# Turning the scan's normalised rows over DRAM and VectorE instead of TensorE and ScalarE, from batch 3 on

## The chip, the cores and the metric

The kernel runs on one core of one Trainium2 chip. A core has TensorE (PE in the profile, its weight loads PEld), VectorE (DVE), ScalarE (ACT), GpSimd (POOL) and SyncE (SP), which here only issues transfers. The metric is the device time of one execution in microseconds (us); less is better.

## The reference

All numbers are float32; x has 8 batches of 512 tokens of 256 features. Four blocks follow each other, each on a layer norm and added back to x. Cut to what matters:

```python
def _layernorm(x, axis=-1, eps=1e-05):
    m = jnp.mean(x, axis=axis, keepdims=True)
    v = jnp.var(x, axis=axis, keepdims=True)
    return (x - m) / jnp.sqrt(v + eps)
...
def _L0_attn_a_ref(x, Win, bin_, Bp, Cp, Dp, Wout, bout):   # the scan
    xi = jax.nn.silu(x @ Win + bin_)
    def step(h, xt):
        h = h * DECAY + xt[:, :, None] * Bp[None, :, :]
        y = jnp.einsum('bij,ji->bi', h, Cp) + Dp * xt
        return (h, y)
    ...
    return y @ Wout + bout
...
x = x + _L0_attn_a_ref(_layernorm(x), ...)   # scan
x = x + _L0_ffn_ref(_layernorm(x), ...)      # shared experts, and 4 of 16 experts for each token
x = x + _L0_attn_b_ref(_layernorm(x), ...)   # causal attention, 16 heads
x = x + _L0_ffn_ref(_layernorm(x), ...)
```

The scan's product x @ Win sums over the 256 features, so on TensorE the normalised rows must stand with features on the partitions. That turning of rows is what this case is about.

## The kernel before, in words

The program has four stages, one after the other: a stretch of the scan with the router and the shared experts of the first mixture (0 to about 337 us in the profile), the routed experts of that mixture (to about 730), a stretch of the attention with the second mixture's router and shared experts (to about 1223), and the routed experts again.

A stretch (function stretch) runs over batches. Work is written as pieces, generators that yield how many TensorE columns each step takes. beside() interleaves pieces by their progress; timed() places steps of a piece at given fractions of the batch. This sets the order in which instructions are recorded; the build then lays each engine's instructions into a queue, which the engine works through in order. SP's transfers wait at the head of SP's queue in the same way.

In iteration b of the scan stretch stand side by side:

- main(b) of the scan: four products of the turned rows with Win (pz_s, L563), each followed by Silu on ScalarE (L572), the scan on VectorE (L574), a scaling on ScalarE (L575) and a VectorE sum (L578), then the product with Wout (py_s, L510) and the addition to x on VectorE (L519);
- for batch b − 1: the norm of the mixture (L468, L469, L487, L493 on VectorE, a power on POOL, L488), its turning on TensorE (pt_m, L430), the router's product (pl_m, L669), the choice of experts on VectorE (L695 to L784, with a product pr_m at L747), and, one batch later still, 16 scatters on POOL (L798), each ahead of which ScalarE makes one column of row numbers (L795);
- the shared experts of earlier batches: pg_m (L1146), Silu (L1164), a VectorE product (act_m, L1165), pd_m (L1174), a ScalarE copy (L1182) and a store on SP (L1184);
- for batch b + 1: the norm (steps at 0.32 to 0.44 and 0.56 to 0.64 of the batch) into a tile xn, and turn(b + 1), two steps at the fractions layer.turns;
- on SP the load of x for batch b + 2 (L149), six loads of expert weights and a store of zeros (L235 to L237, L348, L351), the store of x of batch b − 1 (L1444) and the store of the shared experts.

The first use of the turned rows of batch b + 1 is L563, at the start of iteration b + 1.

There are two ways to turn rows. turned() (L418) transposes each 128 x 128 block on TensorE against the identity into PSUM (pt_l, L430) and copies it to SBUF (L432), for the scan on ScalarE, one half of the features per step. by_shares() (L435) stores the rows to DRAM (L440), loads them back in four shares so that each 32 x 32 block stands in the partitions where it belongs (L443), all in its first step; in its second step VectorE transposes the 32 x 32 blocks in two halves (L452). Before the change by_shares is used in the attention stretch, from batch 2 on.

Of the kernel before, what the change touches and what calls it, by code (L numbers as in the profile page):

```python
# [82 lines left out]
def tile_hybrid_block(  # L83
# [334 lines left out]
    def turned(src, tag: str, into, copies, home=None, past=None):  # L418

        rows = src()  # L420
        if home is None:
            dst = work.tile([P, KD, T], FP, tag="kb4", name=f"xT_{tag}", bufs=KB)
        else:
            dst = home(f"xT_{tag}")
        into(dst)
        for k in range(KD):
            pt = bank([P, NT, P], f"pt_{tag}_{k}")
            for t in range(NT):
                with tc.issue_after(past[-1].ins) if past else nullcontext():
                    nc.tensor.transpose(pt[:, t, :], rows[:, t, :].rearrange("p (q k) -> p k q", k=KD)[:, k], ident)  # L430
            flat = pt.rearrange("p t q -> p (t q)")
            copies[k](dst[:, k, :], flat)  # L432
            yield T // 2

    def by_shares(src, tag: str, into, into_rows: bool, home=None):  # L435


        rows = src()
        through = dram.tile([T, D], FP, name=f"through_{tag}")
        nc.sync.dma_start(out=through.rearrange("(t p) d -> p t d", p=P), in_=rows)  # L440
        share = rows.rearrange("p t d -> p (t d)") if into_rows else kb4(f"share_{tag}").rearrange("p t d -> p (t d)")
        for a in range(QUAD):
            nc.sync.dma_start(  # L443
                out=share[a * SQ : (a + 1) * SQ, :].rearrange("s (g c) -> s g c", g=T // SQ),
                in_=through[:, a * KD * SQ : (a + 1) * KD * SQ].rearrange("(g s) c -> s g c", s=SQ),
            )
        yield 0
        dst = home() if home else work.tile([P, KD, T], FP, tag="kb4", name=f"xT_{tag}", bufs=KB)
        into(dst)
        for half in range(2):  # L450
            g = slice(half * T // SQ // 2, (half + 1) * T // SQ // 2)
            nc.vector.transpose(  # L452
                dst.rearrange("p k (g s) -> p k g s", s=SQ)[:, :, g],
                share.rearrange("p (g i k) -> p k g i", i=SQ, k=KD)[:, :, g],
            )
        yield 0

    by_both = (nc.scalar.copy, nc.vector.tensor_copy)
    by_scalar = (nc.scalar.copy, nc.scalar.copy)
# [60 lines left out]


    class Scan:
        mixture, ahead, copies, turns = 0, 1, by_scalar, (0.75, 0.79)
        quota = (10, 10, 20)
        over, sent, begun_last = 4, 0, 4
        early = 0


# [671 lines left out]
    class Attention:  # L1200
        mixture, ahead, copies, turns = 1, 2, by_both, (0.65, 0.85)
        quota = (10, 8, 20)
        over, sent, begun_last = 0, 4, 8
        early = 2
        norms, scores, choose = (0.0, 0.12, 0.2, 0.28), (0.29, 0.45, 0.55, 0.6), (0.66, 0.95)
        last_rows, last_scores = (0.2, 0.28), (0.35, 0.38)
# [214 lines left out]
    def stretch(layer):  # L1421


        i = layer.mixture
# [7 lines left out]
            return normed(b, f"l{i}_{b}", place, False, first)  # L1432

        def turn(b: int, copies=layer.copies):
            if i == 1 and b >= layer.ahead:
                return by_shares(lambda: xn.pop(b), f"l{i}_{b}", lambda xnT: xT.update({b: xnT}), True)
            return turned(lambda: xn.pop(b), f"l{i}_{b}", lambda xnT: xT.update({b: xnT}), copies)

# [20 lines left out]
        for b in range(layer.ahead):  # L1459
            if b < layer.early:  # L1460
                xT[b] = ready.pop(b)
            else:
                layer.load(b)
                first = i == 0 and b == 0
                issue(Piece(0, norm(b, first)))
                issue(Piece(0, turn(b)))
            if b == 0 and i == 1:
                issue(project(b))

        def first_two():  # L1470

            second = norm(1, True)
            issue(Piece(0, some(second, NT)))
            for _ in range(2):
                pending.pop(0)()
            issue(Piece(0, second))
            load_shared()
            with tc.issue_after(powers["l0_1"].ins):
                for make in late:
                    make()  # L1480
            layer.load(1)
            with tc.issue_after(powers["l0_1"].ins):
                issue(project(0))
            main = layer.main(0, made.pop(0))
            issue(Piece(0, some(main.steps, FIRST)))
            issue(Piece(0, turn(1)))
            issue(Piece(0, some(main.steps, NI - FIRST)))
            issue(project(1))
            second = layer.main(1, made.pop(1))
            issue(Piece(0, some(second.steps, NI)))  # L1490
            issue(main)
            keep_busy(5, "between")
            return Piece(second.columns - NI * KD * T, second.steps)
# [9 lines left out]
        for b in range(1 if begun else 0, B):  # L1503
# [3 lines left out]
            scores, choose, turns = layer.scores, layer.choose, layer.turns  # L1507
            if i == 0 and b == 1:

                scores, choose, turns = (0.95, 0.955, 0.97, 0.975), (0.98, 0.99), (0.96, 0.965)  # L1510
# [35 lines left out]
            if nxt < B:  # L1546
                added = layer.load(nxt)
                if added is not None:
                    pieces.append(timed(added, 0.31, 0.34))
                stats = 0.36 if added is not None else 0.32  # L1550
                pieces += [
                    timed(norm(nxt), *spread(stats, 0.44, NT), *spread(0.56, 0.64, NT)),
                    timed(turn(nxt), *turns),
                ]
# [133 lines left out]
```

## Time and profile before

| | us |
|---|---|
| median of 10 runs | 1616.78 (1612.17 to 1618.53) |
| the profiled execution's own time | 1619.3 |
| its span in the trace | 1617.6 |
| scan stretch, 0 to 340: PE busy / mean granted clock | 324.10 / 0.98 |
| routed experts, 340 to 730: PE busy / clock | 389.77 / 1.00 |
| attention stretch, 730 to 1225: PE busy / clock | 479.11 / 0.99 |
| routed experts, 1225 to 1617: PE busy / clock | 376.30 / 0.99 |

All times inside the kernel are of the profiled execution, counted from the start of its span. The profile names a line of the program by L and its number, and an operation by out<-in. In a timeline row stand the start, the length, the engine, the line, the operation and its tiles, how many were merged (x8), and in brackets how long the engine had been idle and who ended that. A product of the program appears as two to four matmuls there. The granted clock is the share of TensorE's full speed that the chip granted.

### The profile page before, as it was taken

How to read it: one execution, taken by the hardware profiler on the slowest of the kernel's cores; microseconds unless marked ns; L12 is line 12 of the kernel's file. 1: busy time of each engine (PE TensorE's matmuls, PEld its weight loads, DVE VectorE, ACT ScalarE, POOL GpSimd, SP SyncE). 2: the span in 40 equal slices, each digit the busy share in tenths (PEclk: the TensorE clock that was granted, in tenths of full speed). 3: DMA queues.
4: the chain of work that ended last, by engine and by line, in shares of the span. 5: the costliest groups of instructions: out<-in, count | busy, mean ns of one | idle time of the engine just before them, and what ended most of it. 6: DMA issues, size and time to landing. Idle time of an engine off the chain costs nothing. (4 is left out here: it accounts for less than half of the span.)

```text
span 1617.6 us, 34092 instructions
## 1 busy us (share of the span) xinstructions
PE 1569.3 (97%) x10030; PEld 1158.6 (72%) x10030; DVE 1003.1 (62%) x3264; ACT 779.4 (48%) x1622; POOL 771.9 (48%) x639
## 2 busy tenths in 40 slices
PE   8899999999999999999899999999999999999996
PEld 5466665689999999983354454544558999999995
DVE  6877765444466444437888888878844444545453
ACT  3343443245555555546554554454224555555553
POOL 4376655635556555550014422433533555555554
PEclk9999999999999999999999999999999999999998
DMA  5354423557777766641233434342745767777776
GB/s 171 120 202 148 153 104 133 185 92 106 121 123 105 107 97 98 95 66 40 79 89 99 141 96 119 101 123 98 276 146 92 108 115 128 120 137 132 137 133 135
DMA packets 282766, 196.88 MB, mean 122 GB/s; under 512 B 168689, under 2 KB 262673, under 8 KB 282577
## 3 DMA queue, kind: packets, MB, share of 16 engines
q1 hardware_dynamic: 230016, 121.50, 29.0%
q0 software_dynamic: 51984, 72.09, 24.6%
q8 instruction: 85, 1.39, 0.4%
q10 hardware_dynamic: 576, 1.05, 0.2%
q14 instruction: 105, 0.85, 0.2%
HBM read 91.29 MB, written 103.23 MB: 120 GB/s over the span
## 5 line engine op out<-in xcount | busy, mean ns | idle before, releaser
L1073 POOL DMA_INDIRECT part<-rows x272 | 426.3, 1567 | 341.6 <-ACT rows L1072 260.1
L798 POOL DMA_INDIRECT xg<-sorted_m,slots_m x256 | 269.0, 1051 | 246.1 <-ACT slots_m L795 120.6
L1033 PEld LDWEIGHTS ph<-rows,gate 128*128 128x128 f32 x2160 | 277.6, 191 | 32.7 <-ACT rows L1016 22.6
L1033 PE MATMUL ph<-rows,gate 128*128 128x128 f32 x2160 | 291.7, 278 | 0.5 <-ACT rows L1016 0.5
L1033 PE MATMUL ph<-rows,up 128*128 128x128 f32 x2160 | 285.3, 275 | 0.0
L1063 PE MATMUL pyr<-w_all,rows 128*128 x1088 | 279.5, 380 | 1.4 <-DVE rows L1043 1.4
L1033 PEld LDWEIGHTS ph<-rows,up 128*128 128x128 f32 x2160 | 262.9, 192 | 0.0
L1006 DVE COPY up<-w_all 128x512 f32 x270 | 119.9, 445 | 226.3 <-PE ph L1033 210.9
L1006 ACT COPY gate<-w_all 128x512 f32 x270 | 166.4, 617 | 124.2 <-PE ph L1033 120.3
L1043 DVE TENSOR_TENSOR rows<-ph,rows 128x256 f32<-128x256 f32 x272 | 115.4, 424 | 155.2 <-PE ph L1033 142.1
L1295 ACT ACTIVATE w_all<-ps_a 128x1024 f32<-128x1024 f32 x160 | 155.2, 1021 | 105.4 <-PE ps_a L1285 101.3
L1063 PEld LDWEIGHTS pyr<-w_all,rows 128*128 128x128 f32 x1088 | 186.7, 192 | 15.8 <-DVE rows L1043 1.6
L1072 ACT ACTIVATE rows<-pyr,gain 128x256 f32<-128x256 f32 x272 | 128.6, 473 | 78.5 <-PE pyr L1063 61.9
L1041 ACT ACTIVATE rows<-ph 128x256 f32<-128x256 f32 x272 | 104.3, 383 | 117.2 <-PE ph L1033 106.2
L1174 PE MATMUL pd_m<-sd_sb,act_m 128*128 128x256 f32 x512 | 119.7, 383 | 2.2 <-DVE act_m L1165 1.3
L1174 PEld LDWEIGHTS pd_m<-sd_sb,act_m 128*128 128x128 f32 x512 | 96.1, 190 | 26.4 <-issue 8.8
L1285 PE MATMUL ps_a<-w_all 32*128 32x384 f32 (+3 forms) x1024 | 103.4, 467 | 11.5 <-ACT w_all L1295 11.4
L1305 DVE SCALAR_TENSOR_TENSOR w_all<-w_all,causal 128x512 f32<-128x512 f32 (+1 forms) x160 | 91.7, 573 | 26.4 <-ACT w_all L1295 25.5
L1146 PE MATMUL pg_m<-w_all,sg_sb 128*128 128x512 f32 x192 | 92.6, 604 | 0.0
L1146 PE MATMUL pg_m<-w_all,su_sb 128*128 128x512 f32 x192 | 92.6, 605 | 0.0
L1285 PEld LDWEIGHTS ps_a<-w_all 32*128 32x128 f32 x1024 | 45.1, 186 | 66.1 <-ACT w_all L1295 37.5
L1321 PE MATMUL po_a<-w_all,v_a 128*32 128x512 f32 (+3 forms) x1024 | 89.3, 449 | 0.0
(222 smaller groups left out, 1915.5 us busy)
## 6 DMA issues: line engine op xcount, KB each, us to landing
rows<-xg SPq DMA_DIRECT2D x720, 32.0 KB
rows<-xg SPq DMA_DIRECT2D x92, 134.0 KB
part<-x SPq DMA_DIRECT2D x16, 512.0 KB
w_all<-in_L_ffn_gate_w_dram SPq DMA_DIRECT2D x29, 256.0 KB
w_all<-in_L_ffn_up_w_dram SPq DMA_DIRECT2D x29, 256.0 KB
w_all<-in_L_ffn_down_w_dram SPq DMA_DIRECT2D x29, 256.0 KB
part<-ys_m SPq DMA_DIRECT2D x14, 512.0 KB
sum<-part SPq DMA_DIRECT2D x14, 512.0 KB
```

Source lines behind the costliest of these rows:

```text
L798: nc.gpsimd.indirect_dma_start(out=xg[i], out_offset=bass.IndirectOffsetOnAxis(ap=slots[:, at : at + 1], axis=0), in_=rows[:, t, :], in_of ...
L1006: copy(here, w_all[:, bass.ds(held[n][0] + half * KD * F, KD * F)])
L1033: nc.tensor.matmul(ph[s][:, f * P : (f + 1) * P], lhsT=both[s][:, k * F + f * P : k * F + (f + 1) * P], rhs=rows[:, ROW + k * P : ROW + (k ...
L1041: nc.scalar.activation(act, ph[0], AF.Silu)
L1043: made = nc.vector.tensor_mul(act, ph[1], act)
L1063: nc.tensor.matmul(py, lhsT=act[:, f * P : (f + 1) * P], rhs=w_all[:, bass.ds(w + 2 * KD * F + f * D, D)], start=(f == 0), stop=(f == KF - 1),
L1072: nc.scalar.mul(y, py, gain[:, TK : TK + 1])
L1073: acc = nc.gpsimd.indirect_dma_start(out=parts[i][n % 2], out_offset=bass.IndirectOffsetOnAxis(ap=rows[:, D + 2 * TK : D + 2 * TK + 1].bit ...
L1146: made = nc.tensor.matmul(dst, lhsT=w[:, k, f * P : (f + 1) * P], rhs=xnT[:, k, :], start=(k == 0), stop=(k == KD - 1),)
L1174: nc.tensor.matmul(py[:, j, :], lhsT=acts[n][:, f, t * P : (t + 1) * P], rhs=shared[n][3][:, f, :], start=(n == 0 and f == 0), stop=(n == ...
L1285: nc.tensor.matmul(ps[j // 2][:, j % 2, col : col + n], lhsT=k_sb[w][r, o, c * P : (c + 1) * P], rhs=q_sb[r, o, c * P : T], start=True, st ...
L1295: nc.scalar.activation(es[two], ps[two], AF.Exp, scale=ATT_SCALE)
```

## The change

Class Scan gets turns (0.66, 0.92) in place of (0.75, 0.79), and both classes an attribute through, the first batch that goes over DRAM: 3 for the scan, 2 for the attention, where it was layer.ahead = 2 before. So nothing changes in the attention. In the scan, batches 3 to 7 (turned in iterations 2 to 6) use by_shares: the store and the four loads at 0.66 of the iteration, the VectorE transposes at 0.92. The shares are loaded into the tile xn itself (into_rows is True). Batches 0 to 2 are turned as before; the turns of batch 2 have fractions of their own.

```diff
     class Scan:
-        mixture, ahead, copies, turns = 0, 1, by_scalar, (0.75, 0.79)
+        mixture, ahead, copies, turns = 0, 1, by_scalar, (0.66, 0.92)
         quota = (10, 10, 20)
         over, sent, begun_last = 4, 0, 4
+        through = 3
         early = 0
...
         over, sent, begun_last = 0, 4, 8
+        through = 2
         early = 2
...
         def turn(b: int, copies=layer.copies):
-            if i == 1 and b >= layer.ahead:
+            if b >= layer.through:
                 return by_shares(lambda: xn.pop(b), f"l{i}_{b}", lambda xnT: xT.update({b: xnT}), True)
             return turned(lambda: xn.pop(b), f"l{i}_{b}", lambda xnT: xT.update({b: xnT}), copies)
```

In the built program the queues of TensorE, ScalarE and SP differ only by the instructions that go or come, POOL's is the same. On VectorE some pairs of neighbours also change places (L519 and L739, L469 or L487 and L1165). The two VectorE transposes of batches 3 to 7 stand directly ahead of the first scan (L574) of their batch:

```
batch 4, VectorE's queue after the change
L731 pick_m_2<-sorted_m_2,numbers
L519 x<-py_s_1,x
L739 sel_m_2<-pick_m_2
L468 stats_m_3<-x (two)
L469 mv_m_3<-stats_m_3
L1165 act_m_1_1<-pg_m_1_1_1_1,sig_m_1_1_1
L469 mv_m_3<-stats_m_3
L487 rstd_m_3<-mv_m_3
L487 rstd_l_5<-mv_l_5
L452 xT_l_4<-xn_4 (two)
L574 state_s_0<-decay,xi_s_0
```

(Line numbers are those of the kernel before; the change adds a line each ahead of L526 and L1204.)

## The prediction, made before the result was known

> **What bounds the kernel now.** I read the page first: TensorE (PE) is busy through almost the whole span, no other engine is near it.
>
> ```profile
> PE 1569.3 (97%) x10030; PEld 1158.6 (72%) x10030; DVE 1003.1 (62%) x3264; ACT 779.4 (48%) x1622; POOL 771.9 (48%) x639
> ```
>
> An average over stages decides nothing about one of them, and the chain that ended last reaches back only to 1223 us, far behind the scan. So I took the windows of the scan, one for about each of the batches that change (us, then busy us of PE, PEld, DVE, ACT, POOL, granted clock, DMA share, GB/s):
>
> ```profile
> 100.00:125.00 25.00, 25.00 (x102) 15.10 (x101) 18.42 (x70) 12.04 (x30) 18.10 (x20) 1.00 0.56 187
> 125.00:150.00 25.00, 25.00 (x105) 15.98 (x104) 16.46 (x42) 10.69 (x27) 15.62 (x15) 1.00 0.47 160
> 150.00:175.00 25.00, 25.00 (x88) 15.41 (x87) 22.20 (x80) 9.78 (x24) 15.73 (x18) 1.00 0.31 109
> ```
>
> TensorE never stops here: from 77 to 210 us the list of waits has no PE wait. So TensorE time removed is time won, but every stop of TensorE that is added counts in full as well. Whether one is added is read where a batch ends. For batch 4 the timeline of PE gives (start, length, line):
>
> ```profile
> 118.34 1.11 PE L430 MATMUL pt_l<-ident,xn 128*128 128x128 f32 x8
> 119.29 1.89 PE L510 MATMUL py_s<-w_scan,y_s 128*128 128x256 f32 x8
> 121.02 1.88 PE L1146 MATMUL pg_m<-w_all,sg_sb 128*128 128x512 f32 x4
> 122.74 1.89 PE L510 MATMUL py_s<-w_scan,y_s 128*128 128x256 f32 x8
> 124.46 1.88 PE L1146 MATMUL pg_m<-w_all,su_sb 128*128 128x512 f32 x4
> 126.18 1.88 PE L563 MATMUL pz_s<-xT_l,w_scan 128*128 128x512 f32 x4
> ```
>
> The first row is what the change takes out; the last one, L563, is the first reader of the turned rows, 7.84 us later. At the same moment VectorE (DVE) does this:
>
> ```profile
> 124.43 0.58 DVE L739 TENSOR_REDUCE sel_m<-pick_m 128x64 f32<-128x256 f32 x1
> 124.93 0.68 DVE L519 TENSOR_TENSOR x<-py_s,x 128x512 f32<-128x512 f32 x1
> 125.64 0.75 DVE L468 BATCH_NORM_STATS2 stats_m<-x 128x6 f32<-128x256 f32 x2
> 126.31 0.30 DVE L469 BATCH_NORM_AGGREGATE mv_m<-stats_m 128x2 f32<-128x6 f32 x2
> 126.65 0.17 DVE L487 TENSOR_SCALAR rstd_m<-mv_m 128x4 f32<-128x4 f32 x1
> 126.73 0.69 DVE L1165 TENSOR_TENSOR act_m<-pg_m,sig_m 128x512 f32<-128x512 f32 x1
> 127.33 0.16 DVE L487 TENSOR_SCALAR rstd_l<-mv_l 128x4 f32<-128x4 f32 x1
> 128.82 1.23 DVE L574 TENSOR_TENSOR_SCAN state_s<-decay,xi_s 128x512 f32<-128x512 f32 x1 [1.32 <-ACT xi_s L572]
> ```
>
> It has no idle time from 116.83 to 127.49: the expert choice of the batch before, the sums and their statistics. TensorE is already in L563 by then. That is harmless now, and it is where I expect the change to hurt.
>
> **What goes.** Five batches (3 to 7) lose eight PE transposes and two ScalarE copies each. The transposes of batch 4 hold PE from 118.34 to 119.29, 0.95 us; the other batches' rows give the same. 5 x 0.95 = 4.75 us. The copies (group L432, 587 ns each, 5.9 us in all) are worth nothing: ScalarE is busy 10 to 12 us in 25, and no PE wait names it here.
>
> **What is added.** On VectorE two stream transposes per batch; the pair stands at 1.30 us in the attention stage (771.35), with the same tiles. On the SP queue a 512 KB store and four loads of 128 KB, each with its wait. Behind them on SP stand the store of x (L1444), in three batches the next stores and loads; L1444 waits for L519 (90.9 us in batch 3) anyway, so nothing there becomes late that TensorE reads.
>
> **Do the shares land in time?** The rows xn are complete at 110.76 in batch 4 (77.8, 146.1, 179.3, 213.1 in batches 3, 5, 6, 7). But SP has just issued eight transfers, some 2.2 MB (106.82 to 111.18), and the DMA share is 0.95 to 1.05 from 108 to 116, 0.35 after. I place the store behind that. From store to first load the attention stage needs 3.05 us on quiet queues (761.44 to 764.49) and 7.62 behind other loads (783.13 to 790.75); from first load to the end of the VectorE wait 4.9 (790.75 to 795.66). Batch 4: 116 + 3.05 + 4.9 = 124, or 111.2 + 7.62 + 4.9 = 123.7. VectorE comes to the transposes only at 127.5, so the transfer is hidden by 3.5 us. In batches 5 and 6 the share falls at 152 and 186, which gives 160 and 194, 2 to 3 us before VectorE. Batch 7 meets idle queues. Batch 3 is the tight one: the share stays high until 88, so 96 at the latest; 81.1 + 7.62 + 4.9 = 93.6 at the earliest. VectorE is free at 94.53 there, since the constants of L213 stand in front. I take 95.0.
>
> **Where VectorE's turn comes.** VectorE runs its queue in order, and the built program fixes it: in batches 4 to 6 the pair stands behind L519, L739, L468, L469, L1165 and both L487, directly ahead of the scan L574. L1165 itself needs the TensorE group directly ahead of L563 (batches 4 to 7). So TensorE finishes, waits for L1165, the small ones and the pair, and only then starts. Nothing stands between on TensorE's queue to fill it. With 1.30 us for the pair and 0.05 for the release, L563 starts:
>
> - batch 3: 95.0 + 1.35 = 96.35, was 92.11: +4.2
> - batch 4: 127.49 + 1.35 = 128.84, was 126.18: +2.7
> - batch 5: 162.88 + 1.35 = 164.2, was 160.28: +3.9 (here VectorE is slower by some 1.3 at 151.5 to 153.5, while POOL adds at L550; it may move)
> - batch 6: 195.76 + 1.35 = 197.1, was 194.37: +2.7
> - batch 7: 231.02 − 0.95, as L1165 waits for TensorE here, + 1.35 = 231.4, was 230.04: +1.4
>
> Sum +14.9, the 0.95 saved per batch already inside. VectorE's chain starts from TensorE's pl_m and py_s of the same batch, ahead of the removed row, so each batch pays anew and the shifts add.
>
> **The clock.** The idle time before L563 would be 5.2, 3.6, 4.9, 3.7 and 2.3 us. What follows an idle TensorE is in the trace (PE rows, then windows):
>
> ```profile
> 76.33 1.42 PE L430 MATMUL pt_m<-ident,sorted_m 128*128 128x128 f32 x6 [2.65 <-DVE sorted_m L493]
> 78.00:79.00 1.00, 1.00 (x2) 0.00 (x0) 0.00 (x0) 0.78 (x5) 0.69 (x2) 0.50 0.66 105
> 275.15 2.31 PE L430 MATMUL pt_m<-ident,sorted_m 128*128 128x128 f32 x8 [1.62 <-DVE sorted_m L493]
> 277.00:278.00 1.00, 1.00 (x4) 0.59 (x3) 0.00 (x0) 0.73 (x3) 0.00 (x0) 0.50 0.00 0
> ```
>
> After 2.65 us idle the clock is 0.50 from 77.8 to 81.2; after 1.62 us it is 0.50 from 275.8 to 279.2; after 1.31 us (210 to 211.3) it stays at 1.00; after 4.15 us (804.8 to 809.0) it is low from 808 to 815. Half speed for 3.4 us costs 1.7. Bounds: 0 per batch, and 3.4 (two such stretches). I take 1.5, nearest to the single stretch, part of which may fall into the idle time: 5 x 1.5 = 7.5.
>
> The Trainium skill, "TensorE: Matmul & The Clock Gate", section "HAM oscillation — how this bites in real kernels", tells to avoid PE idle gaps above about 3.4 us. By it only four of the five idle times would be punished and this term would be near 6.8; the 1.62 us row here shows a shorter one punished. The same page, "Part 4: PE-mode transpose", gives about 275 ns for a transpose in a kernel's context, by which an estimate of the saving would be 40 x 0.275 = 11 us; this trace has eight in 0.95 us, and that decides.
>
> **Sum.** +14.9 + 7.5 = 22.4. Back comes part of the 1.31 us at 210 (TensorE waits there for VectorE's L1165, which gains on a slowed TensorE), 0 to 1.3, taken as 0.7: +21.7. From 340 us on TensorE is full again (389.8 of 390 us) and nothing is changed, so the shift arrives at the end. The profiled execution took 1619.3 us (span 1617.6), giving 1641.0; it stands 2.5 above the median 1616.78, so the median becomes 1638.5.
>
> **Rivals.**
> - A, idle without a slow clock: the stops are as above, but TensorE keeps 1.00, as after the 1.31 us. 14.9 − 0.7: 1631. Against it: 1.62 and 2.65 us.
> - B, the shares land late: POOL's scatters use the DMA engines at the same time (POOL 15 to 18 us busy in 25), and if each round trip takes 7.62 + 4.9 after the burst instead of 3.05 + 4.9, the pair starts at 100.5 in batch 3 instead of 95.0, at 128.5, 164.5 and 198.5 in 4 to 6 instead of 127.5, 162.9 and 195.8: 5.5 + 1.0 + 1.6 + 2.7 = 10.8 more, 1649. For it: batch 3 has no margin at all.
> - C, faster: VectorE gets to the pair before TensorE gets to L563, then only the 4.75 us remain: 1612. It decides at 123.9 in batch 4 (125.23 − 1.35), 3.6 us before VectorE is free. The built queue speaks against it; only a VectorE much ahead of this trace would do it.
> - D, nothing measurable (within 0.2%, 3.2 us, about what this measurement can tell): stops of about 1 us each, which the 0.95 pays: 1617. It needs VectorE free 2.5 us earlier. That the change doesn't do what it says is excluded: the built program has 40 PE transposes and ten copies less, and ten VectorE transposes, five stores and twenty loads more.
>
> **Chances.** Forecast 0.64 (1632 to 1645), A 0.15 (1624 to 1632), B 0.12 (up to 1652), C 0.05, D 0.04. Range 1624 to 1650: it leaves out C, D and the end of B. Faster 0.05, same 0.04, slower 0.91.
>
> **What would show it.** Right: in the list of waits a new PE wait of L563 for DVE xT_l L452, five times, 2 to 5 us each, 17 to 20 in all; granted clock 0.50 for 3.4 us behind most of them; VectorE's L452 without a DMA wait in batches 4 to 7. Wrong: L452 waiting for DMA in all batches (B), L563 starting without idle time (C), or clock 1.00 throughout (A). The prediction falls if the batches' shifts don't add, that is if TensorE had slack behind L563 that the trace hides.

## The result, and the profile after

The changed kernel took **1641.56 us** (median of 8 runs, 1639.14 to 1643.71); the kernel before took 1616.71 beside it. The ratio is **1.0156, 95% interval 1.0147 to 1.0165**: slower by 24.9 us, where +21.7 was predicted. The profiled execution took 1638.05 us (span 1636.3). In the changed kernel L563 is L564, L574 is L575, L1165 is L1166.

The first line of the page shows that the intended removal happened (40 PE transposes less, ten ScalarE copies less, ten VectorE instructions more), and that PE was busy for longer all the same:

```profile
PE 1574.5 (96%) x9990; PEld 1156.1 (71%) x9990; DVE 1007.7 (62%) x3274; ACT 775.1 (47%) x1612; POOL 771.8 (47%) x639
```

Fewer instructions and more busy time mean slower instructions. Two of the three windows shown of before (PE, PEld, DVE, ACT, POOL, granted clock, DMA share, GB/s) show where:

```profile
125.00:150.00 25.00, 21.56 (x70) 13.15 (x69) 17.27 (x54) 6.99 (x18) 11.81 (x12) 0.93 0.24 78
150.00:175.00 25.00, 20.53 (x80) 12.30 (x80) 15.70 (x62) 7.01 (x20) 14.92 (x17) 0.89 0.70 233
```

PE stops for 3.4 and 4.5 us in windows where it never stopped, and the granted clock (third number from the end) falls below 1.00. The end of batch 4 in the timeline of PE:

```profile
126.36 1.88 PE L1147 MATMUL pg_m<-w_all,su_sb 128*128 128x512 f32 x4
131.68 2.82 PE L564 MATMUL pz_s<-xT_l,w_scan 128*128 128x512 f32 x3 [3.44 <-DVE xT_l L452]
```

L564 now waits 3.44 us for VectorE's transposes, and even then three of its matmuls take 2.82 us, where four took 1.88 before. VectorE in the same moments:

```profile
127.44 0.68 DVE L519 TENSOR_TENSOR x<-py_s,x 128x512 f32<-128x512 f32 x1
...
129.26 0.66 DVE L1166 TENSOR_TENSOR act_m<-pg_m,sig_m 128x512 f32<-128x512 f32 x1
...
130.22 1.30 DVE L452 STREAM_TRANSPOSE xT_l<-xn 128x512 f32<-128x512 f32 x2
```

No row carries an idle time in brackets: VectorE runs through, and the pair's turn comes last. The list of PE's waits from 60 to 300 us sums it up for the five batches (us, times, longest):

```profile
PE pz_s L564 <- DVE xT_l L452: 17.7, 5, 4.5
```

The single idle times are 4.46, 3.44, 4.47, 3.19 and 2.18 us (batches 3 to 7). Windows of 3.4 us from the start of each batch's first L564 show the clock, here batches 4 and 7:

```profile
131.70:135.10 3.40, 3.40 (x4) 1.38 (x5) 0.00 (x0) 0.00 (x0) 0.69 (x1) 0.51 0.00 0
...
249.10:252.50 3.40, 3.40 (x8) 1.54 (x9) 0.68 (x1) 0.69 (x1) 0.00 (x0) 1.00 0.02 5
```

Batches 3, 5 and 6 read 0.50 too. Four of the five stops are followed by half clock, four matmuls in the time of eight; behind the two longest it lasts on, to 97.6 and 176.1.

### The profile page after: what moved, and what is told of

It reads as the page before. It is cut to its first block, busy times and chain, and to the rows that moved or that the text cites. A ratio compares the mean times of both kernels' runs of the same rounds, so it can differ in the third digit from the quotient of the medians.

```text
span 1636.3 us, 34063 instructions
## 1 busy us (share of the span) xinstructions
PE 1574.5 (96%) x9990; PEld 1156.1 (71%) x9990; DVE 1007.7 (62%) x3274; ACT 775.1 (47%) x1612; POOL 771.8 (47%) x639
## 5 line engine op out<-in xcount | busy, mean ns | idle before, releaser
L1064 PEld LDWEIGHTS pyr<-w_all,rows 128*128 128x128 f32 x1088 | 186.8, 192 | 15.8 <-DVE rows L1044 1.6
```

The lines of the kernel that those rows point to most:

```text
L1064: nc.tensor.matmul(py, lhsT=act[:, f * P : (f + 1) * P], rhs=w_all[:, bass.ds(w + 2 * KD * F + f * D, D)], start=(f == 0), stop=(f == KF - 1),
```

## The experiments

Theories as in the prediction: **VectorE's queue** (the pair's turn comes late, TensorE stops, the clock falls), against **the transfer** (store and shares cost by landing late, B) and **no slow clock** (A). All variants differ from the changed kernel in the scan stretch only; added lines shift the numbers, so L564 appears as L568 to L579 and L452 as L455 to L463. The kernel before was timed beside each group, as chips differ: 1637.61 us for the first four runs, 1617.95 for the next four, 1616.77 for the last four. So ratios are compared, not times.

| run | median, us | ratio to before, 95% interval | as us |
|---|---|---|---|
| not turned at all | 1632.43 | 0.9967 (0.9954 to 0.9980) | −5.4 |
| transfer alone | 1645.20 | 1.0038 (1.0019 to 1.0056) | +6.2 |
| VectorE pair alone, late | 1655.90 | 1.0109 (1.0088 to 1.0131) | +17.9 |
| changed, idle time partly filled | 1656.41 | 1.0129 (1.0104 to 1.0154) | +21.1 |
| changed kernel again | 1642.24 | 1.0154 (1.0133 to 1.0175) | +24.9 |
| changed, idle time filled | 1632.10 | 1.0091 (1.0070 to 1.0112) | +14.7 |
| shares first and pair earlier | 1615.96 | 0.9989 (0.9976 to 1.0001) | −1.8 |
| rows early, pair in VectorE's gap | 1631.76 | 1.0086 (1.0065 to 1.0107) | +13.9 |
| shares first only | 1641.28 | 1.0146 (1.0125 to 1.0167) | +23.6 |
| pair earlier only | 1633.43 | 1.0098 (1.0078 to 1.0118) | +15.8 |
| from batch 6 on | 1624.59 | 1.0042 (1.0027 to 1.0058) | +6.8 |
| shares first, pair earlier, not batch 6 | 1613.16 | 0.9978 (0.9966 to 0.9990) | −3.6 |

The last column is (ratio − 1) times the group's kernel before.

### Not turned at all

```diff
+            if i == 0 and b >= layer.through:
+                return unturned(b)
```

(unturned gives L564 the tile xn as it lies)

> Batches 3 to 7 of the scan are not turned at all: TensorE's transposes, the copies, the store, the loads and VectorE's transposes are all left out, and L563 reads the normalised rows as they lie. It prices what the change removes. My theory (the wait for VectorE's queue costs everything, the removed transposes are worth 0.95 us a batch): 4.75 us under the kernel before, so about 1612 (1610.5 to 1613.5), no wait of L564 on TensorE's list and no half clock from 77 to 290 us. Rival (the gain is smaller since something else, such as VectorE's scores or act, ends the batch in any case): 1615 to 1617.

Measured −5.4 us (−7.5 to −3.3), and no wait of L564. The removed work is worth about what the prediction took, 4.75. Half clock was not gone altogether: 6.83 us of it stand from 254.17, behind a wait of 4.44 us of pr_m for sel_m that all four profiles of this group have (see the last section).

### The transfer alone

```diff
         yield 0
+        if tag[:3] == "l0_":
+            into(share.rearrange("p (k q) -> p k q", k=KD))
+            yield 0
+            return
```

> As the changed kernel, but VectorE's two transposes are left out in batches 3 to 7: the store and the four loads stay, and TensorE reads the loaded shares as they land. My theory (VectorE's queue position, not the transfer): TensorE waits only where the shares land behind it, in batch 3 (90.5 against 87.7 us, 2.8 idle and perhaps 1.7 of slow clock) and batch 5 (0.75): 1616.8 - 4.75 + 3.6 to 5.3 = 1615.6 to 1617.3. Rival, the transfer and what it crowds out on the DMA engines is the cost: about 1638 to 1642, as the changed kernel.

Measured +6.2 us (3.1 to 9.2): neither. The ten executions lie between 1638.2 and 1649.6 us, and the profiled one took 1648.9, so its waits may be above the typical ones. The waits of PE from 60 to 300 us:

```profile
PE pz_s L568 <- DMA xn<-through_l: 6.3, 2, 5.1
...
PE pd_m L1179 <- DVE act_m L1170: 3.7, 1, 3.7
```

In batch 3 TensorE waits 5.1 us for the shares, more than the 2.8 I had from the trace of after, and the wait for act_m (1.3 in the changed kernel) is 3.7: act_m stands in VectorE's queue behind a norm that waited 1.79 us for a scatter, until 215.91. That TensorE runs into this because nothing held it up earlier is argued, not tried. So the transfer alone is not the 25 us, but it is not free either.

### VectorE's pair alone, late

```diff
+        if tag[:3] != "l0_":
             nc.sync.dma_start(out=through.rearrange("(t p) d -> p t d", p=P), in_=rows)
...
+            if tag[:3] == "l0_":
+                behind_all(made)
```

(the four loads likewise; behind_all queues the pair behind the last 60 recorded instructions of VectorE)

> The other half alone: no store and no loads in batches 3 to 7, VectorE's two transposes read the normalised rows directly (so the rows between the quarters of partitions are not exchanged: that part of the turning is left out), and they are tied to the end of VectorE's queue, three small instructions (0.38 us) earlier than in the changed kernel in batches 4 to 7 and 2.7 us earlier in batch 3 (ahead of the constants of L213). My theory: idle before L564 is 4.46 - 2.7, 3.44 - 0.38, 4.47 - 0.38, 3.19 - 0.38, 2.18 - 0.38 = 13.5 us, slow clock 5 to 8 us, so 1633.5 to 1637. Rival, the transfer is the cost: 1612 to 1617, since no transfer is left.

Measured +17.9 us (14.4 to 21.5), with no store and no loads of the rows at all. The waits of PE:

```profile
PE pz_s L577 <- DVE mv_m L482: 11.6, 3, 4.6
...
PE pz_s L577 <- DVE xT_l L463: 2.7, 1, 2.7
...
PE pz_s L577 <- issue: 2.3, 1, 2.3
```

The same stop of the same line, 16.6 us in five waits (13.5 expected), named by other neighbours in VectorE's queue: in batch 4 the pair ends at 127.93 and L577 starts at 128.07. Most of the loss is there without a byte of the rows moved; the transfer theory falls as the main cause.

### TensorE's idle time filled, in part and wholly

```diff
+    FILL = {3: 15, 4: 11, 5: 15, 6: 10, 7: 6}     # second run: 17, 13, 17, 12, 8
...
+                if b in FILL:
+                    keep_busy(FILL[b], tag)
                 for c in range(NI):
```

> The changed kernel with 15, 11, 15, 10 and 6 fp32 matmuls of ones by ones (0.256 us each by the rows ahead of the second batch) put on TensorE directly ahead of the first L564 of batches 3 to 7, where it sits idle for 4.46, 3.44, 4.47, 3.19 and 2.18 us: 3.8, 2.8, 3.8, 2.6 and 1.5 us of work of no use, inside the idle time. Nothing else differs. My theory (the idle time is followed by half clock, 8.6 us in all): the waits stay, the half-clock stretches behind them go: 1641.6 - 8.6 = 1633 (1631.5 to 1635). Rival, the slow clock costs nothing or comes from something else than TensorE's idle time: 1641 or more.

> As the first run with matmuls of ones in TensorE's idle time, with more of them: 17, 13, 17, 12 and 8 ahead of the first L564 of batches 3 to 7 (4.4, 3.3, 4.4, 3.1 and 2.0 us), which leaves idle pieces under 1.5 us. In the first such run pieces of 2.05, 2.90 and 3.14 us were left, and two of the four half-clock stretches with them. My theory: no half clock behind L564 at all, the waits of VectorE's transposes as before in sum, so 8.6 us under the changed kernel of this group, that is 15 to 18 us over the kernel before. Rival, the slow clock is not a cost: as the changed kernel, 24 to 26 us over.

The first gave +21.1 (17.0 to 25.2), which lies between the two expectations and decides nothing. The second ran beside the changed kernel:

> The changed kernel itself, once more, beside the others of this group: chips differ (the kernel before took 1637.6 us on the one of the first group, 1616.7 on the one of the result), so each group has to be read against its own kernel before. Every theory: 24 to 26 us over the kernel before (ratio 1.0147 to 1.0165), with five waits of L564 of 16 to 19 us in sum.

The changed kernel again: +24.9, as in the result, with 20.1 us in five waits, 2.4 more than in the first profile (batch 3 has 7.08 us in place of 4.46, as the pair there waited 2.1 us for the shares). With the idle time filled: +14.7, so 10.1 us less by the medians, 1642.24 − 1632.10. Windows from the first L568 of batches 4 and 7 in that profile:

```profile
132.00:135.40 3.40, 3.40 (x12) 2.26 (x13) 0.71 (x1) 0.69 (x1) 0.63 (x1) 1.00 0.00 0
...
243.60:247.00 3.40, 3.40 (x8) 1.52 (x9) 0.70 (x1) 0.69 (x1) 0.00 (x0) 1.00 0.02 5
```

Clock 1.00, as in the windows of the three other batches. The pair is hardly earlier: from the end of the group ahead to L568, fill and waits together, pass 5.33, 3.17, 4.46, 3.26 and 2.18 us, against 7.08, 3.16, 4.48, 3.23 and 2.18 without fill. That is 18.4 against 20.1, and the difference is batch 3 alone. (The 67 products hold PE for 15.8 us, less than the 0.256 us each that I had reckoned with.) So the slow clock is a cost of its own, 8 to 10 us of the 25: 10.1 by the medians, of which up to 1.7 may be batch 3's shorter stop. Rival A falls.

### The two moves, together and apart

Two edits on top of the changed kernel. Shares first: the experts' weights of scan batches from 3 on are loaded behind the shares. Pair earlier: L724 (maxima of the choice), L519 and L1166 are queued behind the pair.

```diff
-                with tc.issue_after(load_x(b + 1).ins):
+                loaded = load_x(b + 1)
+                if b >= self.through:
+                    behind_shares[:] = later[b - 1 :: shares]   # issued behind the last share
+                    return
+                with tc.issue_after(loaded.ins):
...
+            with after_pair():          # likewise around L724 and L1166
+                nc.vector.tensor_add(rows, py, rows)
```

Pair earlier has turns (0.66, 0.8), so that the pair is recorded first.

> All the work of the changed kernel, with two moves. The weights of the experts are loaded behind the shares instead of ahead of the store, and VectorE's pair is tied ahead of L724 (the maxima of the expert choice), the later sum L519 and the later act_m L1166, some 4 us earlier in VectorE's queue. My theory: L564 starts when TensorE gets there, but the pair's 1.3 us now stand ahead of act_m, which the TensorE group behind the first L564 needs, so about 1.1 to 1.7 us of idle time a batch appear there instead, and in batch 3 the shares are late by up to 2.8 us; no half clock or one stretch: 0 to +8 us against the kernel before, likeliest +3.5. Rival, the cost is the transfer wherever VectorE stands: 18 to 26 us over the kernel before.

> One of the two moves of the earlier-pair run alone: the experts' weights are loaded behind the shares, and VectorE's queue stays as the changed kernel has it, the pair directly ahead of the scan L575. My theory (the place in VectorE's queue): 20 to 25 us over the kernel before, with 16 to 18 us of waits of L564 for VectorE; only batch 3, where the shares come as late as VectorE, may gain 0 to 3 us. Rival (the transfer standing behind the weights was the cost): 2 under to 6 over the kernel before.

> The other move alone: VectorE's pair is tied ahead of L724, L519 and L1166 as in the earlier-pair run, the store stays behind the weights on SP's queue as in the changed kernel. Then VectorE reaches the pair before the shares are there (125.7 against 127.3 us in batch 4, 85 against 90.5 or later in batch 3) and stands still with everything behind it. My theory, with VectorE's queue in order: 3 to 6 us of wait of the pair for the transfer in batch 3, 1 to 2 in batches 4 and 5, and act_m late for TensorE by as much; in all 8 to 20 us over the kernel before, likeliest 13. Rival, the transfer costs nothing anywhere: as the earlier-pair run, 2 under. Rival, only the transfer costs: 24 over.

| | weights first | shares first |
|---|---|---|
| pair late | +24.9 | +23.6 |
| pair earlier | +15.8 | −1.8 |

**Both moves** took the whole loss away. Timeline of PE and of VectorE in batch 4:

```profile
120.90 1.88 PE L1161 MATMUL pg_m<-w_all,su_sb 128*128 128x512 f32 x4
122.61 1.88 PE L577 MATMUL pz_s<-xT_l,w_scan 128*128 128x512 f32 x4
```

```profile
119.91 1.30 DVE L458 STREAM_TRANSPOSE xT_l<-xn 128x512 f32<-128x512 f32 x2
```

The pair runs 1.4 us ahead of its reader, and L577 follows the group ahead of it without a stop. My +3.5 was too much: act_m ran at 122.88, straight after its own operand, so the pair cost TensorE nothing there except in batch 6 (3.1 us).

**Shares first only** changed nothing, although SP's queue shows how much earlier the shares are. Store and first load of batch 4, in the changed kernel and here:

```profile
114.77 0.42 SPq L440 DMA_DIRECT2D through_l<-xn  x1
121.92 2.67 SPq L443 DMA_DIRECT2D xn<-through_l  x4
```

```profile
115.66 0.36 SPq L440 DMA_DIRECT2D through_l<-xn  x1
118.73 1.92 SPq L443 DMA_DIRECT2D xn<-through_l  x4
```

From store to load 3.07 us instead of 7.15, and PE's waits are the same:

```profile
PE pz_s L571 <- DVE xT_l L455: 17.9, 5, 4.9
```

**Pair earlier only** moved the wait. From PE's list of waits, and from VectorE's:

```profile
PE pz_s L570 <- DVE best_m L731: 10.8, 4, 3.9
```

```profile
DVE xT_l L455 <- DMA xn<-through_l: 15.0, 4, 5.2
```

VectorE, with its whole queue behind it, now stands 15.0 us in four batches for the shares, and act_m comes late for TensorE as well (3.6 us in one wait). So the pair's place was the cause that showed, and the transfer was right behind it: in the changed kernel the first covered the second.

### From batch 6 on

```diff
-        through = 3
+        through = 6
```

> The change in a smaller dose: the new way only from batch 6 on (batches 6 and 7). My theory, by the two batches' own waits (3.19 and 2.18 us, one half-clock stretch of 1.7 behind the first, none behind the second, less 2 x 0.95): 5.2 us over the kernel before (3.5 to 7). Rival, a like cost for each batch: 2/5 of 24.6 = 9.8 over.

+6.8 (4.4 to 9.4), with L564's waits at 5.4 us in two, as batches 6 and 7 had. The interval holds 5.2 and only just leaves out 9.8; with the waits as forecast, the cost goes by each batch's own stop.

### Rows early, pair in VectorE's gap

```diff
+            if nxt < B and i == 0 and nxt >= layer.through:
+                layer.load(nxt)
+                pieces += [
+                    timed(norm(nxt), *spread(0.02, 0.1, NT), *spread(0.16, 0.24, NT)),
+                    timed(turn(nxt), 0.26, 0.52),
+                ]
...
+        with after_pair():
             nc.vector.transpose(turned_pl, pl)
```

(with shares first, and L519 behind the pair as well)

> All the work of the changed kernel, placed where my theory says it is free: the scan's normalised rows are made at the head of the batch instead of its middle, stored at once, the shares are loaded ahead of the experts' weights, and VectorE's pair is tied directly ahead of L681, where VectorE sits idle for 3 us a batch waiting for TensorE's logits (18.6 us in five waits, 60 to 290 us). My theory: the shares land before that idle time, the pair disappears in it, and what is left is the removed TensorE work: 4.75 us under the kernel before (6 under to 1 under). Rival 1, the transfers cost by themselves: 10 or more over it. Rival 2, the earlier rows delay VectorE's scan and act at the head of the batch: 0 to 8 over it, with waits of L1175 or L510 for VectorE.

Measured +13.9 (10.5 to 17.3): my theory's number failed. VectorE's waits, then PE's:

```profile
DVE stats_l L478 <- DMA x<-in_L_attn_a_x_dram: 17.1, 4, 4.7
DVE xT_l L460 <- DMA xn<-through_l: 7.0, 4, 3.5
```

```profile
PE pt_m L435 <- DVE sorted_m L503: 9.9, 8, 3.7
```

L564 waits no more, but the statistics of the batch behind it, moved forward, stand ahead of the pair and wait there for a load of x; behind them pair, choice and router's rows come late (pr_m 4.1 us in five waits, pd_m 3.4 in one). The pair itself stands 7.0 us for the shares besides. By its number this is rival 1 (the transfers cost by themselves, 10 or more); by its waits it looks more like rival 2, above its range: another instruction of VectorE's queue that comes too early and holds up the rest. The run has both and does not part them.

### Both moves, without batch 6

```diff
-            if b >= layer.through:
+            if b >= layer.through and (i == 1 or b != 6):
...
-                if b >= self.through:
+                if b >= self.through and b != 6:
```

> The earlier-pair run (all of the change's work, shares ahead of the weights, the pair earlier in VectorE's queue), but batch 6 turned by TensorE as before. That run's only new wait of TensorE stood there: 3.11 us at 204.8 us for act_m, where the kernel before has 1.31, and half clock behind it. My theory: 1.8 of wait and 1.7 of slow clock less, 0.95 of transposes more: 2.0 - 2.6 = 4.6 us under the kernel before (6 to 2 under). Rival, the wait comes from elsewhere (POOL's scatters) and stays: 1 under to 1 over.

−3.6 us (−5.5 to −1.6): faster than both kernels, by little. The wait for act_m is back at 1.3 us, what the kernel before has.

## Why the prediction was right, step by step

- **The saving**, 4.75: 5.4 (3.3 to 7.5) when nothing is turned.
- **The place in VectorE's queue**: right, and shown by the pair alone (+17.9) and by moving it. The idle times, predicted 5.2, 3.6, 4.9, 3.7, 2.3, came as 4.46, 3.44, 4.47, 3.19, 2.18: 17.7 instead of 19.7. All five were a little too long.
- **The clock**: predicted 7.5. PE ran at half clock to 97.6, 135.2, 176.1 and 213.7, which from the starts of L564 (92.18, 131.68, 171.22, 210.22) is 5.4, 3.4, 4.9 and 3.4 us, and half of it lost: 8.6. My even 1.5 per batch hid two double stretches and one stop without any. The run with filled idle time puts it at 8 to 10.
- **The shares land in time**: right for the queue as built (no DMA wait of the pair in the first profile, 2.1 us in batch 3 of the second). In the changed kernel's trace the last of the 2048 packets of 256 bytes that bring the shares ends at 90.11, 126.90, 166.96 and 206.41 (batches 3 to 6), and the pair starts at 90.74, 130.22, 169.76 and 208.77. Where the pair stands and waits for the shares (pair earlier only), it starts 0.5 to 0.95 us behind the last packet. So, as an estimate, some 0.2, 2.4, 2.2 and 1.8 us were to spare; the prediction had none, 3.5, 2.9 and 1.8. Of its two sums for batch 4 the second was nearer: SP issues the store at once, and the first load comes 7.15 us later, behind the weights, not 3.05. With the pair placed some 4 us earlier the margin is gone, and it waits.
- **Given back**, 0.7 of the 1.31 us ahead of pd_m: wrong, that wait is still 1.31 (at 228.94).
- **The sum**: 17.7 + 8.6 − 4.75 = 21.6 in the scan's rows, against 19.7 + 7.5 − 4.75 − 0.7 = 21.75 predicted: waits 2 too long and a clock term 1.1 too small met, so part of the closeness is luck. Between like rows, the first pt_m of L430 after 70 us (76.33 before, 72.76 after) and the first ph (337.43, 356.83), the distance grew by 22.97. Of the 1.4 left, 0.8 may be the 0.16 us by which neighbouring matmul rows overlap (1.88 long, 1.72 apart) and which each of the five stops forfeits; that is argued, not tried. The spans of the two profiled executions differ by 18.7 only, as the changed one was 3.6 us ahead at 72.76, where both kernels still do the same work, and won 0.7 behind 356.83. The medians differ by 24.9 (the profiled execution of before stood 2.5 above its median, that of after 3.5 below), 1.9 more than the 22.97; where these lie is open.

## What to carry to other kernels

Work taken from the busiest engine is priced by the place of its replacement in another engine's in-order queue: look for the last instruction ahead of it, what that one waits for, and who reads the result next. When a wait is found, ask which wait lies just under it: here either repair alone brought 1 or 9 of the 25 us, both together 27. And a stop of the matrix engine costs its length and, behind four of the five here, a slow stretch; filling it with idle matmuls shows how much is which.

## What the runs showed of the hardware that was not expected

- The length of a stop alone did not decide about the clock. In the changed kernel 1.52 us (ended at 294.13) was followed by half clock from 295.60 to 299.0, while 2.18 us (249.05) was not; with filled idle time 1.53 us (95.39) was not. The half-clock stretches lasted 3.41 or 6.83 us.

```profile
294.13 2.21 PE L430 MATMUL pt_m<-ident,sorted_m 128*128 128x128 f32 x8 [1.52 <-DVE sorted_m L493]
249.05 1.96 PE L564 MATMUL pz_s<-xT_l,w_scan 128*128 128x512 f32 x4 [2.18 <-DVE xT_l L452]
```

- The Trainium skill, "TensorE: Matmul & The Clock Gate", "Part 1: The HAM clock gate", speaks of a free-running activity window of some 3.4 us. The traces agree: in each of the fourteen profiles all half-clock stretches begin whole multiples of 3.413 us apart (in the changed kernel from 73.73 to 90.80, 131.76, 169.31, 210.26 and 295.60 it is 5, 12, 11, 12 and 25 times). Along this grid the 1.52 us lie in one window, 292.19 to 295.60, and the 2.18 us are split into 0.94 and 1.24. Of the windows at full clock between 60 and 340 us in all profiles, the 38 with 2.0 us or more without a matmul were all followed by half clock, those with under 1.3 us never, and those between in 14 of 41 cases. So where a stop falls in the grid explains most of it, not all; no run set out to move a stop within the grid.
- The kernel before took 1637.6 us on the chip of the first group, 1.3% above the others. All four profiles from there show a wait of pr_m for sel_m of 4.4 to 4.5 us that is 1.1 at most in the other profiles; the rest of the difference was not followed.
